# A decoder kernel: head outputs turned into both partition halves, context keys and values in pairs of row halves, and biases as three bf16 rows

## The chip, the cores and the metric

The kernel runs on one core of a Trainium2 chip. The metric is the device time of one execution in microseconds. The engines are named as in the profile: PE is TensorE's matmul, PEld its weight load, DVE is VectorE, ACT is ScalarE, POOL is GpSimd, SP is SyncE, whose queue issues nearly all the loads. TensorE's clock is throttled by the chip; the profile gives the granted clock as a share of full speed.

## The reference, cut to what matters

The program is a decoder of two layers on `x` of 4 x 256 x 256 fp32 values and a context `ctx` of 4 x 256 x 64. Each layer adds three blocks to `x`, each on a layer norm of it. Layer 0 has a latent attention, a cross attention and a block that works on the tokens a router picks. Layer 1 has a *head attention*, a causal cross attention, and 28 experts of which each token takes six. The change touches the head attention and the context side of the cross attention in layer 1:

```python
# head attention of layer 1: within a token, 16 heads attend to one another
qkv = x @ w_qkv.T + b_qkv                     # x: layer norm of the input, (4, 256, 256)
q, k, v = qkv.reshape(b, n, 3, 16, 16) ...    # (b, n, head, dim)
attn = softmax(einsum('bnhd,bngd->bnhg', q, k) / sqrt(256))
out = einsum('bnhg,bngd->bnhd', attn, v)
out = out.transpose(0, 2, 1, 3).reshape(b, n, c)   # a head's tokens become rows
return out @ w_out.T + b_out

# cross attention of layer 1 (two groups of 512 tokens, 16 heads of 16)
qp = q @ Wq.T
k, v = split(latent_kv @ Wkv_expand.T)        # latent_kv: ctx, 64 values per token
scores = qh @ kh.T / 4, causal; attn = softmax(scores)
return (attn @ vh) @ Wout.T
```

The reshape after the head attention's transpose mixes tokens and heads: row n' = 16 h + q of its result holds head h of the 16 tokens 16 q to 16 q + 15. So the result of all heads of all tokens of a batch row must be turned before the output projection.

## The kernel before, in words

The 1024 tokens lie as eight tiles `x[t]` of 128 rows by 256 values in SBUF through the whole program; each block reads them and adds to them. Blocks are written as Python generators that yield between steps, and `_side_by_side` deals the steps of two of them out in turn, by the numbers of steps that it is given. Each engine then has one in-order queue; within what the data and the buffers allow, the framework's scheduler may set an instruction earlier or later than it was written. PSUM has three rings of two buffers: tag `sc` (two banks each), `tp` and `o`. What takes a buffer of a ring waits until the user before the last has been read out.

*Head attention* (`_head_attention`, L1331 to L1462) works in two halves of four tiles, `half(0)` and `half(1)`. In each half the layer norm is turned into `hT` (L1361 to L1371) with the tokens ordered so that a step j takes 128 tokens whose heads share columns. Then four steps j:

- `project(j)` (L1375): a product of one row, the ones times the bias (L1380), and two of 128 rows (L1382), into a `sc` buffer `pqkv`, for each of two column halves of 384. Two ScalarE copies bring it to `qkv` (L1386).
- `weigh(j)` (L1389): GpSimd multiplies queries by keys, four products of 128 x 1024 (`qk`, L1400). VectorE sums two of them at a time (L1406), takes the maximum and subtracts (L1409, L1410). ScalarE takes the exponential (L1411).
- `combine(j)` (L1414): VectorE divides by the sum, multiplies by the values (`pv`, L1425) and sums into `O` (L1432).

The steps overlap: `weigh(j + 1)` goes before `combine(j)`. After the fourth step `O` holds 16 heads of 4 x 16 values; for each four heads (n = 0 to 3) four fp32 transposes against the identity bring 64 rows each to a `tp` buffer `o_tp` (L1446) and one ScalarE copy of 64 x 512 sorts them into `aoT` (L1448). The output projection of each tile is a one-row bias product (L1453) and four products of 64 rows (L1456) into an `o` buffer `apo`; VectorE adds it to `x` (L1457). There are four such tiles per half.

*Cross attention* (`_cross_attention`, L1465) loads its weights first (L1478 to L1485) in SyncE's queue. `context_kv(bp)` (L1494), once for each half of the tokens, fills `vz` with zeros by two DMAs (L1499), makes four key products of 64 rows by 512 columns (`xpk`, L1502) with a ScalarE copy each into `kz` (L1503), and four value products of 64 rows by 256 columns (`xpv`, L1510), two to a `tp` buffer, with two ScalarE copies to every other column of `vz` (L1515). The queries are `xpq` (L1646) and `xqT` (L1647); scores go to `sc` buffers `xsc`.

The order around the change (L532 to L584): the head attention's loads are issued and its half 0 (`heads_a`) is dealt out beside layer 0's cross attention of the second half of the tokens (`mix`) and the routed block on it; that ends in the `mpb` turns and the update of `x`. Then `heads_a`'s remaining steps and the cross attention of the first tokens are dealt out beside `second()`: eight steps of `heads_b` (half 1 of the head attention), both `context_kv`, and the rest of `heads_b`. After that comes the cross attention of the second tokens, and the experts.

Constants lie in one tile `cst`: the identity, masks, ones and others at columns named `K_...`.

Of the kernel before, what the change touches and what calls it, by code (L numbers as in the profile page):

```python
# [54 lines left out]
K_END = K_LATER + P  # L55
# [52 lines left out]
def kernel(ctx: ExitStack, tc: tile.TileContext, w: dict, out: bass.AP):  # L108
# [310 lines left out]
    for _ in range(4):  # L419
# [17 lines left out]
        blank=blank, psum=psum, sm=sm, cst=cst, ident=ident, identb=identb, maskb=maskb, tri=tri, ones=ones,  # L437
# [550 lines left out]
def _routed_block(nc, w, x, env):  # L988
# [20 lines left out]
    for i in range(4):  # L1009
        nc.gpsimd.tensor_copy(later[:, i], cst[:, K_LATER:K_END])  # L1010

# [319 lines left out]
def _head_attention(nc, tc, x, w, env):  # L1331
# [5 lines left out]
    ident, ones_row, layernorm = (env[n] for n in ("ident", "ones_row", "layernorm"))  # L1337
# [7 lines left out]
    b1qkv = a1.tile([1, 3 * C], F32, name="b1qkv")  # L1345
    nc.sync.dma_start(b1qkv, w["a_bqkv"])
    w1out = a1.tile([4 * D, 4, C], F32, name="w1out")
    nc.sync.dma_start(w1out, w["a_wout"].rearrange("(m p) n -> p m n", p=4 * D))
    b1out = a1.tile([1, C], F32, name="b1out")
    nc.sync.dma_start(b1out, w["a_bout"])  # L1350

    def half(g):
# [22 lines left out]
        def project(j):  # L1375
            qkv = a2.tile([P, 3 * C], F32, tag="qkv", name="qkv")
            pq = psum.tile([P, 2, 512], F32, tag="sc", name="pqkv")
            for i in range(2):
                cols = slice(i * 384, (i + 1) * 384)
                nc.tensor.matmul(pq[:, i, :384], ones_row, b1qkv[:, cols], start=True, stop=False)  # L1380
                for k in range(2):
                    nc.tensor.matmul(  # L1382
                        pq[:, i, :384], hT[:, k, j * P : (j + 1) * P], w1qkv[:, k, cols], start=False, stop=(k == 1)
                    )
            for i in range(2):
                nc.scalar.copy(qkv[:, i * 384 : (i + 1) * 384], pq[:, i, :384])  # L1386
            return qkv
# [54 lines left out]
        oT = a1.tile([4 * D, 4, 2, H, Q], F32, tag="oT", name="aoT")  # L1442
        for n in range(4):
            tp = psum.tile([P, 4, P], F32, tag="tp", name="o_tp")
            for i in range(4):
                nc.tensor.transpose(tp[: 4 * D, i, :], O[:, 4 * n + i].rearrange("p j d -> p (j d)"), ident)  # L1446
            dst = oT[:, :, :, 4 * n : 4 * n + 4, :].rearrange("p m b h q -> p h (m b) q")
            nc.scalar.copy(dst, tp[: 4 * D].rearrange("p h (m q) -> p h m q", q=Q))  # L1448
            yield
        for t in range(4):  # L1450
            b, i = divmod(t, 2)
            po = psum.tile([P, C], F32, tag="o", name="apo")
            nc.tensor.matmul(po, ones_row, b1out, start=True, stop=False)  # L1453
            for m in range(4):
                lhsT = oT[:, m, b, 8 * i : 8 * i + 8, :].rearrange("p h q -> p (h q)")
                nc.tensor.matmul(po, lhsT, w1out[:, m, :], start=False, stop=(m == 3))  # L1456
# [8 lines left out]
def _cross_attention(nc, tc, x, w, env):  # L1465
# [4 lines left out]
    psum, sm, ctxT = (env[n] for n in ("psum", "sm", "ctxT"))  # L1470
# [9 lines left out]
    wxk = c1.tile([LAT, 4, P], F32, name="wxk")  # L1480
    nc.sync.dma_start(wxk, w["c_wk"])
    wxv = c1.tile([LAT, C], F32, name="wxv")
    nc.sync.dma_start(wxv, w["c_wv"])
# [10 lines left out]
    def context_kv(bp):  # L1494
# [5 lines left out]
        for n in range(4):  # L1500
            pk = psum.tile([P, 512], F32, tag="tp", name="xpk")
            nc.tensor.matmul(pk, wxk[:, n], ctxT[:LAT, tok], start=True, stop=True)  # L1502
            nc.scalar.copy(kz[:, n // 2, n % 2, :], pk)  # L1503
            if n % 2:
                yield
        for t in range(0, 4, 2):
            pv = psum.tile([P, 2, C], F32, tag="tp", name="xpv")
            for j in range(2):
                t0 = (4 * bp + t + j) * P
                nc.tensor.matmul(pv[:, j], ctxT[:LAT, t0 : t0 + P], wxv, start=True, stop=True)  # L1510
# [172 lines left out]
def _constants():  # L1683
# [23 lines left out]
    c[:, K_LATER:] = np.where(p[None, :] <= SLOTS + p[:, None] % SLOTS, 0.0, -1e30)  # L1707
# [3 lines left out]
def _laid_out(a):  # L1711


    def row(v):
        return v.reshape(1, -1)
# [42 lines left out]
    o["a_bqkv"] = by_dim(a["L1_attn_b_qkv"].reshape(-1, 1)).reshape(1, -1)  # L1758
    o["a_wout"] = a["L1_attn_w_out"].T
    o["a_bout"] = row(a["L1_attn_b_out"])  # L1760
# [34 lines left out]
```

## Time and profile before

| what | value |
|---|---|
| time, median of 3 runs | 945.69 us (944.62 to 947.14) |
| the profiled execution, its own time | 917.45 us |
| its span, first to last instruction | 915.7 us |
| mean granted TensorE clock | 0.842 |
| VectorE busy, ScalarE busy | 522.6 us (57%), 293.6 us (32%) |

The profiled execution was 28 us shorter than the timed median; its span lacks 1.75 us of its own time.

These are the stages around the change, with the busy time of each engine in them and the granted clock, from the trace:

| stage, us from the start | PE | DVE | ACT | POOL | clock |
|---|---|---|---|---|---|
| 290 to 330: start of heads half 0, mix | 29.1 | 23.1 | 9.4 | 6.3 | 0.64 |
| 330 to 440: heads half 0 beside the routed block | 66.2 | 88.8 | 17.9 | 48.3 | 0.73 |
| 440 to 465: turns of half 0, first step of half 1, first keys and values | 21.3 | 8.5 | 9.4 | 10.9 | 0.84 |
| 465 to 492: output projections, keys and values, second step | 26.7 | 14.0 | 4.1 | 1.0 | 0.50 |
| 492 to 560: steps of half 1 beside the cross attention | 48.4 | 45.2 | 20.4 | 27.6 | 0.75 |
| 560 to 604: end of half 1, its projections | 40.8 | 37.2 | 18.4 | 0.7 | 0.82 |
| 604 to 692: cross attention of the second tokens | 72.8 | 52.0 | 35.6 | 38.0 | 0.82 |

A line of the profile names the instruction's line in the code, engine, operation, output and inputs by the program's names, the shape of the array used for products (64*128: 64 rows, 128 columns), and how many instructions it stands for. An fp32 product is two instructions on TensorE, two passes over the same columns; "x8" for four products is that. In the order of time, `[5.44 <-PE pqkv L1382]` after an instruction says that its engine had been idle for 5.44 us and that the named instruction released it. Idle time of an engine that nothing waits for costs nothing.

### The profile page before, as it was taken

What the parts mean: (1) busy time and instruction counts of PE and PEld (TensorE: products, weight loads), DVE (VectorE), ACT (ScalarE), POOL (GpSimd) and SP (SyncE); (2) the same over time, 40 slices, a digit from 0 to 9 for tenths busy, and PEclk for the clock granted to TensorE, in tenths of its full rate; (3) what the DMA queues carried; (4) which work ended last, traced back from release to release, by engine and by line L of the source; (5) the groups of instructions that cost most, each with busy time, mean ns of one, the idle gap of its engine ahead of it and who ended that gap; (6) DMA issues with size and microseconds to landing.
All of it is one profiled execution on the core that took longest, in us unless ns stands there. A gap on an engine that the chain in (4) does not pass through costs nothing. (4 is left out here: it accounts for less than half of the span.)

```text
span 915.7 us, 11540 instructions
## 1 busy us (share of the span) xinstructions
PE 735.1 (80%) x3594; PEld 460.5 (50%) x3594; DVE 522.6 (57%) x1304; ACT 293.6 (32%) x958; POOL 309.5 (34%) x248
## 2 busy tenths in 40 slices
PE   4999999779988696543988786989696589979990
PEld 2645656445455343331554354656464367757770
DVE  3357467886553578779363678847554323353332
ACT  1245354442441211211220343416431134424430
POOL 2012122214210263740314222023532466646662
PEclk9799999889999678667767677879966889989995
DMA  8769999500505100510300000057216756676655
GB/s 318 208 221 325 325 325 336 216 1 0 184 6 212 59 3 4 180 46 0 124 0 0 1 1 1 1 223 297 79 46 176 213 94 116 110 206 111 111 80 155
DMA packets 84270, 117.03 MB, mean 128 GB/s; under 512 B 5133, under 2 KB 72271, under 8 KB 83696
## 3 DMA queue, kind: packets, MB, share of 16 engines
q1 hardware_dynamic: 71312, 99.46, 33.3%
q0 software_dynamic: 11232, 15.21, 9.8%
q10 hardware_dynamic: 1664, 1.57, 0.5%
q8 instruction: 33, 0.54, 0.2%
q14 instruction: 29, 0.24, 0.1%
HBM read 58.80 MB, written 55.33 MB: 125 GB/s over the span
## 5 line engine op out<-in xcount | busy, mean ns | idle before, releaser
L883 POOL DMA_INDIRECT acc<-ys,xb x62 | 97.8, 1578 | 76.2 <-ACT Tx L839 43.7
L1400 POOL TENSOR_TENSOR qk<-qkv 128x1024 f32<-128x1024 f32 x32 | 74.3, 2352 | 71.9 <-ACT qkv L1386 71.9
L333 POOL TENSOR_TENSOR pr<-pr,rs 128x512 f32<-128x512 f32 x32 | 41.5, 1298 | 162.6 <-DVE rs L331 81.9
L847 PE MATMUL pgu<-wgu_e,Tx 128*128 x248 | 91.9, 496 | 2.9 <-ACT Tx L839 1.6
L323 ACT ACTIVATE pr<-sc,nb 128x256 f32<-128x256 f32 x128 | 59.0, 474 | 60.2 <-DVE nb L318 59.9
L878 PE MATMUL py<-wdn_e,Th 88*128 x248 | 65.2, 389 | 9.8 <-issue 9.3
L1544 ACT ACTIVATE xpr<-xsc,cnm 128x256 f32<-128x256 f32 (+1 forms) x128 | 52.2, 421 | 63.6 <-DVE cnm L1539 50.7
L701 POOL DMA_INDIRECT lists<-R,rows x48 | 46.7, 973 | 59.0 <-DVE rows L685 19.5
L878 PEld LDWEIGHTS py<-wdn_e,Th 88*128 88x128 f32 x248 | 47.7, 195 | 26.2 <-issue 9.8
L1406 DVE TENSOR_REDUCE s<-qk 128x128 f32<-128x2048 f32 x16 | 36.6, 2286 | 42.2 <-POOL qk L1400 42.1
L847 PEld LDWEIGHTS pgu<-wgu_e,Tx 128*128 128x128 f32 x248 | 45.2, 202 | 20.5 <-issue 4.1
L853 DVE TENSOR_TENSOR eh<-pgu,sg 128x176 f32<-128x176 f32 x62 | 21.1, 340 | 51.3 <-ACT sg L851 51.3
L93 PE MATMUL av<-pT,ckt 128*64 128x256 f32 x256 | 40.5, 412 | 8.7 <-DVE pT L349 8.5
L314 DVE TENSOR_REDUCE nm<-sc 128x4 f32<-128x1024 f32 x32 | 38.9, 1217 | 13.1 <-PE sc L93 13.0
L882 ACT ACTIVATE ys<-py,wsel 128x256 f32<-128x256 f32 x62 | 29.4, 475 | 48.7 <-PE py L878 45.7
L867 DVE SCALAR_TENSOR_TENSOR wjunk<-cst,e_all,xb 128x28 f32<-128x28 f32 x62 | 15.2, 247 | 49.6 <-ACT ys L882 48.7
L851 ACT ACTIVATE sg<-pgu 128x176 f32<-128x176 f32 x62 | 19.7, 318 | 73.9 <-PE pgu L847 73.9
L93 PE MATMUL xsc<-kz,xqT 32*128 32x256 f32 (+1 forms) x256 | 37.5, 402 | 7.3 <-ACT xpr L1544 4.3
L96 PE MATMUL tp<-cst,pr 128*128 128x128 f32 x256 | 38.7, 293 | 3.3 <-DVE pT L349 2.4
L93 PE MATMUL sc<-ckv,qk 64*128 64x256 f32 x256 | 39.3, 405 | 1.5 <-ACT qk L301 0.7
L96 PE MATMUL x_tp<-cst,xpr 128*128 128x128 f32 x192 | 36.2, 322 | 4.3 <-DVE xpT L1560 2.6
L96 PEld LDWEIGHTS tp<-cst,pr 128*128 128x128 f32 x256 | 29.8, 148 | 17.4 <-issue 14.1
(334 smaller groups left out, 1529.4 us busy)
## 6 DMA issues: line engine op xcount, KB each, us to landing
lists<-blank SPq DMA_DIRECT2D x9, 3600.0 KB, 28.1
wgu_e<-in_e_gu_dram SPq DMA_DIRECT2D x4, 2464.0 KB, 25.6
xb<-lists SPq DMA_DIRECT2D x62, 144.0 KB, 2.9
acc<-blank SPq DMA_DIRECT2D x5, 1152.0 KB, 11.6
wdn_e<-in_e_dn_dram SPq DMA_DIRECT2D x4, 1232.0 KB
wq<-in_m_wq_dram SPq DMA_DIRECT2D x4, 1024.0 KB, 11.3
mwo<-in_m_wo_dram SPq DMA_DIRECT2D x2, 2048.0 KB
part<-acc SPq DMA_DIRECT2D x16, 256.0 KB, 3.2
```

Of the source, the lines that this page charges most:

```text
L93: self._next(self.engine.matmul(*args, **kw))
L96: self._next(self.engine.transpose(*args, **kw))
L314: nc.vector.tensor_reduce(nm, sc, AX.X, ALU.max, negate=True)
L323: nc.scalar.activation(pr[:, e, qt, :], sc[:, e, qt, :], AF.Exp, bias=nb[:, e, qt : qt + 1], accum_out=ss[:, e, qt : qt + 1],)
L333: nc.gpsimd.tensor_tensor(pr[:, 1], pr[:, 1], rs[:, 1].unsqueeze(2).to_broadcast([P, 2, S]), ALU.mult)
L701: put = nc.gpsimd.indirect_dma_start(out=lists, out_offset=bass.IndirectOffsetOnAxis(ap=rows[:, i, n : n + 1], axis=0), in_=R[:, i, :], in ...
L847: nc.tensor.matmul(pg, xT[:, k, :], self.wgu[:, bass.ds(e * (4 * M) + k * 2 * M, 2 * M)], start=(k == 0), stop=(k == 1))
L878: nc.tensor.matmul(py, hT[:, k, :], self.wdn[:, bass.ds(e * (2 * C) + k * C, C)], start=(k == 0), stop=(k == 1))
L883: nc.gpsimd.indirect_dma_start(out=accs[self.puts % len(accs)], out_offset=bass.IndirectOffsetOnAxis(ap=xb[:, C : C + 1].bitcast(I32), axi ...
L1400: nc.gpsimd.tensor_tensor(pr[:, 4 * i : 4 * i + 4], q3[:, h0 : h0 + 4].unsqueeze(2).to_broadcast([P, 4, H, D]), k3.unsqueeze(1).to_broadca ...
L1406: nc.vector.tensor_reduce(s[:, hh], pr, AX.X, ALU.add)
L1544: nc.scalar.activation(pr[:, j, cols], sc[:, j, cols], AF.Exp, bias=nm[:, i, j : j + 1], accum_out=ss[:, i, h : h + 1])
```

## The change

It has three parts.

*The turn and the output projection.* Each head group of `O` is multiplied twice, as fp32 matrix products instead of transposes: by the identity into partitions 0 to 63 of `o_tp` and by a new constant, the identity with its columns rolled by 32 (`turned32`, 128 more columns of `cst`), into partitions 64 to 127. So both partition halves hold the turned heads, the upper half with the column blocks moved by 32. Two ScalarE copies of 128 rows (one per m) instead of one of 64 sort them into an `aoT` of 128 rows, and the output projection is two products of 128 rows instead of four of 64. `w1out` is loaded to match.

*Biases.* Both bias vectors are one array of 1024 values, loaded as 128 x 8. VectorE rounds it to bf16, subtracts, rounds the rest, subtracts and rounds again: three bf16 parts. Three DMAs write them to DRAM, one reads them back as three rows of 1024. The bias product is then three bf16 rows of ones (`onesb`) against three bf16 rows of bias, in both projections.

*Context keys and values.* The context and the two weights are loaded twice, into partitions 0 to 63 and 64 to 127 (six loads in place of two; `ctxT`, loaded at the start, stays for layer 0). Products alternate between the two halves, so that two in a row use different rows of the array. They take `sc` buffers, two banks each, instead of `tp`; keys are copied two products at a time.

```diff
-K_END = K_LATER + P
+K_TURN = K_LATER + P
+K_END = K_TURN + P
...
-    b1qkv = a1.tile([1, 3 * C], F32, name="b1qkv")
-    nc.sync.dma_start(b1qkv, w["a_bqkv"])
-    w1out = a1.tile([4 * D, 4, C], F32, name="w1out")
-    nc.sync.dma_start(w1out, w["a_wout"].rearrange("(m p) n -> p m n", p=4 * D))
-    b1out = a1.tile([1, C], F32, name="b1out")
-    nc.sync.dma_start(b1out, w["a_bout"])
+    bias = a1.tile([P, 8], F32, name="b1")
+    nc.sync.dma_start(bias, w["a_b"].rearrange("(p c) -> p c", p=P))
+    b1 = a1.tile([3, 4 * C], BF16, name="b1rows")
+    scratch = env["stack"].enter_context(tc.tile_pool(name="b1d", bufs=1, space=DRAM)).tile([3, 4 * C], BF16, name="b1d")
+    for i in range(3):
+        part = a1.tile([P, 8], BF16, name=f"b1part{i}")
+        nc.vector.tensor_copy(part, bias)
+        if i < 2:
+            nc.vector.tensor_tensor(bias, bias, part, ALU.subtract)
+        nc.sync.dma_start(scratch[i].rearrange("(p c) -> p c", p=P), part)
+    nc.sync.dma_start(b1, scratch)
+    onesb = a1.tile([3, P], BF16, name="onesb")
+    nc.vector.tensor_copy(onesb, env["ones"][:3])
+    b1qkv, b1out = b1[:, : 3 * C], b1[:, 3 * C :]
+    w1out = a1.tile([P, 2, C], F32, name="w1out")
+    nc.sync.dma_start(w1out, w["a_wout"].rearrange("(m p) n -> p m n", p=P))
...
-                nc.tensor.matmul(pq[:, i, :384], ones_row, b1qkv[:, cols], start=True, stop=False)
+                nc.tensor.matmul(pq[:, i, :384], onesb, b1qkv[:, cols], start=True, stop=False)
...
-        oT = a1.tile([4 * D, 4, 2, H, Q], F32, tag="oT", name="aoT")
+        oT = a1.tile([P, 2, 2, H, Q], F32, tag="oT", name="aoT")
         for n in range(4):
             tp = psum.tile([P, 4, P], F32, tag="tp", name="o_tp")
             for i in range(4):
-                nc.tensor.transpose(tp[: 4 * D, i, :], O[:, 4 * n + i].rearrange("p j d -> p (j d)"), ident)
-            dst = oT[:, :, :, 4 * n : 4 * n + 4, :].rearrange("p m b h q -> p h (m b) q")
-            nc.scalar.copy(dst, tp[: 4 * D].rearrange("p h (m q) -> p h m q", q=Q))
+                head = O[:, 4 * n + i].rearrange("p j d -> p (j d)")
+                nc.tensor.matmul(tp[: 4 * D, i, :], head, ident, start=True, stop=True)
+                nc.tensor.matmul(tp[4 * D :, i, :], head, env["turned32"], start=True, stop=True)
+            for m in range(2):
+                dst = oT[:, m, :, 4 * n : 4 * n + 4, :].rearrange("p b h q -> p h b q")
+                src = tp[:, :, m * 2 * 32 : m * 2 * 32 + 32].rearrange("p h (b q) -> p h b q", q=Q)
+                nc.scalar.copy(dst, src)
             yield
         for t in range(4):
             b, i = divmod(t, 2)
             po = psum.tile([P, C], F32, tag="o", name="apo")
-            nc.tensor.matmul(po, ones_row, b1out, start=True, stop=False)
-            for m in range(4):
+            nc.tensor.matmul(po, onesb, b1out, start=True, stop=False)
+            for m in range(2):
                 lhsT = oT[:, m, b, 8 * i : 8 * i + 8, :].rearrange("p h q -> p (h q)")
-                nc.tensor.matmul(po, lhsT, w1out[:, m, :], start=False, stop=(m == 3))
+                nc.tensor.matmul(po, lhsT, w1out[:, m, :], start=False, stop=(m == 1))
...
-    wxk = c1.tile([LAT, 4, P], F32, name="wxk")
-    nc.sync.dma_start(wxk, w["c_wk"])
-    wxv = c1.tile([LAT, C], F32, name="wxv")
-    nc.sync.dma_start(wxv, w["c_wv"])
+    ctx2 = c1.tile([P, B * S], F32, name="ctx2")
+    wxk = c1.tile([P, 4, P], F32, name="wxk")
+    wxv = c1.tile([P, C], F32, name="wxv")
+    for dst, src in ((wxk, "c_wk"), (wxv, "c_wv"), (ctx2, "ctxT")):
+        for e in range(2):
+            nc.sync.dma_start(dst[e * LAT : (e + 1) * LAT], w[src])
...
-        for n in range(4):
-            pk = psum.tile([P, 512], F32, tag="tp", name="xpk")
-            nc.tensor.matmul(pk, wxk[:, n], ctxT[:LAT, tok], start=True, stop=True)
-            nc.scalar.copy(kz[:, n // 2, n % 2, :], pk)
-            if n % 2:
-                yield
+        for g in range(2):
+            pk = psum.tile([P, 2, 512], F32, tag="sc", name="xpk")
+            for e in range(2):
+                half = slice(e * LAT, (e + 1) * LAT)
+                nc.tensor.matmul(pk[:, e], wxk[half, 2 * g + e], ctx2[half, tok], start=True, stop=True)
+            nc.scalar.copy(kz[:, g], pk)
+            yield
         for t in range(0, 4, 2):
-            pv = psum.tile([P, 2, C], F32, tag="tp", name="xpv")
+            pv = psum.tile([P, 2, 512], F32, tag="sc", name="xpv")
             for j in range(2):
                 t0 = (4 * bp + t + j) * P
-                nc.tensor.matmul(pv[:, j], ctxT[:LAT, t0 : t0 + P], wxv, start=True, stop=True)
+                half = slice(j * LAT, (j + 1) * LAT)
+                nc.tensor.matmul(pv[:, j, :C], ctx2[half, t0 : t0 + P], wxv[half], start=True, stop=True)
+            pv = pv[:, :, :C]
...
-    c[:, K_LATER:] = np.where(p[None, :] <= SLOTS + p[:, None] % SLOTS, 0.0, -1e30)
+    c[:, K_TURN:] = np.roll(np.eye(P), -(P // 4), 1)
+    c[:, K_LATER:K_TURN] = np.where(p[None, :] <= SLOTS + p[:, None] % SLOTS, 0.0, -1e30)
```

More of the change, by code (lines that the diff above doesn't have):

```diff
@@ L436 @@
     env = dict(
-        blank=blank, psum=psum, sm=sm, cst=cst, ident=ident, identb=identb, maskb=maskb, tri=tri, ones=ones,
+        turned32=cst[:, K_TURN:], blank=blank, psum=psum, sm=sm, cst=cst, ident=ident, identb=identb, maskb=maskb, tri=tri, ones=ones,
         ones_row=ones_row, layernorm=layernorm, ln_stats=ln_stats, ln_apply=ln_apply, rsqrt=rsqrt, transposed=transposed, ctxT=ctxT, neghalf=neghalf,
@@ L1009, in _routed_block @@
     for i in range(4):
-        nc.gpsimd.tensor_copy(later[:, i], cst[:, K_LATER:K_END])
+        nc.gpsimd.tensor_copy(later[:, i], cst[:, K_LATER:K_TURN])
     kT = ms1.tile([P, HK, 2 * SLOTS], F32, name="mkT")
@@ L1336, in _head_attention @@
     psum, sm = env["psum"], env["sm"]
-    ident, ones_row, layernorm = (env[n] for n in ("ident", "ones_row", "layernorm"))
+    ident = env["ident"]
     H = D = 16
@@ L1465, in _cross_attention @@
 def _cross_attention(nc, tc, x, w, env):
-    psum, sm, ctxT = (env[n] for n in ("psum", "sm", "ctxT"))
+    psum, sm = env["psum"], env["sm"]
     ident, identb, maskb, ln_apply, transposed = (env[n] for n in ("ident", "identb", "maskb", "ln_apply", "transposed"))
@@ L1757, in _laid_out @@
     o["a_wqkv"] = by_dim(a["L1_attn_w_qkv"]).T
-    o["a_bqkv"] = by_dim(a["L1_attn_b_qkv"].reshape(-1, 1)).reshape(1, -1)
+    o["a_b"] = np.concatenate([by_dim(a["L1_attn_b_qkv"].reshape(-1, 1)).ravel(), a["L1_attn_b_out"]])
     o["a_wout"] = a["L1_attn_w_out"].T
-    o["a_bout"] = row(a["L1_attn_b_out"])
     o["c_wq"] = a["L1_xattn_Wq"].T
```

## The prediction

> **What bounds the kernel now.** I read first the page's busy table and its 40 slices (22.9 us each), to see which stages the change touches and what is full there.
>
> ```profile
> PE 735.1 (80%) x3594; PEld 460.5 (50%) x3594; DVE 522.6 (57%) x1304; ACT 293.6 (32%) x958; POOL 309.5 (34%) x248
> ...
> PE   4999999779988696543988786989696589979990
> ...
> DVE  3357467886553578779363678847554323353332
> ...
> PEclk9799999889999678667767677879966889989995
> ```
>
> The touched lines run from 289 to 604 us (slices 13 to 26). There TensorE's granted clock is mostly 0.6 to 0.8, and no engine is full throughout: VectorE leads before 440, TensorE from 440 to 490. So the stage must be read by waits. For the tile `qkv` (what each engine waited for, who waited):
>
> ```profile
>   PE pqkv L1382: 31.2, 6
> ...
>   POOL qk L1400: 71.9, 7
> ...
>   DVE s L1406: 42.1, 14
> ```
>
> GpSimd's products (four of 2.33 us per step) start when ScalarE has copied a projection, and VectorE's sums follow them. A late projection therefore holds GpSimd, then VectorE. Third, the order of time around the two longest such waits:
>
> ```profile
> 465.29 2.07 PE L1502 MATMUL xpk<-ctxT,wxk 64*128 64x512 f32 x2 [2.90 <-ACT vz L1515]
> ...
> 473.56 3.78 PE L1456 MATMUL apo<-w1out,aoT 64*128 64x256 f32 x8
> ...
> 480.12 3.78 PE L1456 MATMUL apo<-w1out,aoT 64*128 64x256 f32 x8
> ...
> 487.11 1.64 PE L1380 MATMUL pqkv<-b1qkv,cst 1*128 1x384 f32 x2
> ...
> 491.73 0.86 ACT L1386 COPY qkv<-pqkv 128x384 f32<-128x384 f32 x2 [5.44 <-PE pqkv L1382]
> ...
> 499.60 0.68 DVE L1647 TENSOR_SCALAR xqT<-xpq 128x512 f32<-128x512 f32 x1
> ...
> 510.48 1.64 PE L1380 MATMUL pqkv<-b1qkv,cst 1*128 1x384 f32 x2
> ...
> 519.52 0.86 ACT L1386 COPY qkv<-pqkv 128x384 f32<-128x384 f32 x2 [5.93 <-PE pqkv L1382]
> ...
> 520.46 9.20 POOL L1400 TENSOR_TENSOR qk<-qkv 128x1024 f32<-128x1024 f32 x4 [18.52 <-ACT qkv L1386]
> ```
>
> From 465 to 491 TensorE works without a gap and everyone waits: GpSimd stands from 461 to 492.7 but for 1 us, VectorE is half idle. The queue is in order, so the second projection of heads half 1 and the front of the next block stand behind output projections and context keys. And it runs at half clock, as the stretches show (busy us of PE, PEld, DVE, ACT, POOL; clock; DMA share):
>
> ```profile
> 456.00:460.00 4.00, 4.00 (x21) 2.96 (x20) 2.29 (x1) 3.07 (x6) 4.00 (x3) 1.00 0.00 0
> ...
> 472.00:476.00 4.00, 4.00 (x9) 2.47 (x9) 2.25 (x2) 0.59 (x1) 0.00 (x0) 0.50 0.00 0
> ...
> 480.00:484.00 4.00, 4.00 (x10) 3.14 (x10) 0.12 (x2) 0.00 (x0) 0.00 (x0) 0.50 0.00 0
> ```
>
> **The change, part by part** (gains negative; times are those of the profile before).
>
> *Prices.* A 384-column fp32 product is two passes of 0.64 us at half clock or 0.32 at full; 256 columns 0.43 or 0.21; 512 columns 0.85 or 0.43 (start-to-start in the rows above and their neighbours). A bf16 product is one pass, and by the mask row (128x512 bf16, 0.38 us alone, pipeline included) a quarter of the stream: 0.32 us for 384 columns at half clock where fp32 took 1.6. Products in two row halves: eight 64*128 passes of 256 columns of the first attention's scores go in 1.06 us start to start, where 8 x 0.213 is 1.7, so 1.6 times as fast. In two column halves (av, 128*64): eight in 1.02, 1.7 times.
>
> *A. Bias rows, 289 to 323.* New on SyncE's queue: one bias load for two, three writes to DRAM, one read back. The third write is issued when VectorE has made the third row. VectorE's six small operations stand between the layer norms at 298 to 301 and cost 0.07 to 0.17 each (rows of such size), about 0.6 in all. The second half of the wq load now stands behind those writes: 302 instead of 292.7, and first needed at about 362, so its cover is 50 us. Write and read back: 2.8 us each by wxv's landing, plus at most 3.1 for the wq half in front (1 MB at 336 GB/s, the highest slice): rows ready at 308 to 311. In the new order the first bias product stands after psim (about 311) and before transposes that wait until 316 to 319. Hidden; without this cover each us late stands in TensorE's queue 1:1. What is gained: the old bias products stood earlier, and held the transposes behind them:
>
> ```profile
> 301.74 2.92 PE L1380 MATMUL pqkv<-b1qkv,cst 1*128 1x384 f32 x4
> ...
> 304.60 1.54 PE L468 MATMUL h_tp<-cst,h 128*128 128x128 f32 x6
> ```
>
> Their inputs were there at 301.6, so up to -2.9; less 0.6 of VectorE, and the psim behind them ran at full clock already at 310 and may now fall into the half-clock part (+0.4 to +1.7). I take -2.0 (ends -2.5 and 0).
>
> *B. First projection, 322 to 330.* One bias at half clock, 1.6 to 0.3, lies between the transposes and qkv at 329.79, which starts GpSimd's first eight products: -1.3.
>
> *C. 330 to 440.* The scheduler also moves one `qk` product ahead of a rotation on GpSimd. One side: sums earlier by 2 us; other side: the routed block's third turn later by 1.7. VectorE orders both; -0.5 (ends -1 and +2).
>
> *D. o_tp and the first projection of half 1, 444 to 452.* Each turn becomes two fp32 products of two passes, 128 columns each: 16 passes for 4. By av's 1.7, 16 x 0.107 / 1.7 = 1.0 us at full clock for 0.43, four times a half. Seven of the eight products of n=0 stand ahead of the projection, at half clock: +1.2, less the bias's 0.5: +0.7. ScalarE's aoT copies become 16 of 128 elements: 0.25 us by the 128x128 kv copy (0.27) for 8 x 0.58, equal in sum.
>
> *E. 452 to 500.* The stall 461 to 465 stays: ScalarE's exp at 464.29 waits for GpSimd's products, vz copies stand behind it, and key and value products now share the "sc" buffers, whose third user waits for those copies. From 465.3 before: 40 fp32 passes and 6 bias passes, 26.1 us. After: xpk one pair 4 x 0.85 / 1.6 = 2.1; apo 8 x 0.43 = 3.4 (two row groups for four); xpv 8 x 0.43 / 1.6 = 2.1; pqkv 8 x 0.64 = 5.1 (none is done ahead now); four biases 1.1; gaps 1.2: 15.0 at half clock. The projection ends at 480.4 for 491.4: -11. Not all of it is path: in GpSimd's new order two of its products (4.7) precede cln_rs, and VectorE's order puts two sums (2.3 each) ahead of hT and xqT. Following it through: copy 481.4, two products 486.1, cln_rs 487.1, four products 491.7, sum 494.0, hT 494.7, first half of xpq 496.4, xqT 497.1 for 499.6 to 500.3: -3.1, with one sum done beforehand. If the clock is full from about 470, the projection ends at 475 and xqT comes at 491.7: -8.6. I take -6.
>
> Here two rules of the Trainium skill are weighed. "TensorE: Matmul & The Clock Gate", Part 1, has the clock full after one busy window of about 3.4 us. The rows differ: 26 us busy at 0.50 from 465 on, full only after projections and transposes of all 128 rows; while 448 to 460, entered through such products, is at 1.00. By the page the clock would be full from 469 whatever the change, 26.1 would have been about 15, and E would be worth some 3; by the rows E's work at half clock is real, and full-row products (apo, paired keys) may end it sooner. I go by the rows. "TensorEngine Tiling (Array Packing)", Key Properties, says that a change of tiling mode drains the array, which speaks against the change: between the first o_tp and xpq I count 29 changes of mode for 20, and o_tp cuts one key pair apart. The rows price it: xpk 453.74 follows o_tp and pqkv that began at 452.53 with 1.07 us of streaming, so about 0.1 per change: +1, within E's gap term.
>
> *F. Third projection, 508 to 520.* Two biases at half clock, 3.2 to 0.6, ahead of the copy that GpSimd awaits 18.5 us: -2.6. *G.* The fourth, at full clock: -1.3, but VectorE is full from 560 to 580: 0.
>
> *H. Tail, 581 to 604.* VectorE's last sum of O ends at 583.8; then TensorE is the path to x_in at 603.56. At full clock: four output projections of 1.7 become 0.85 (-3.4), biases 4 x 0.6 to 0.15 (-1.8), o_tp +0.6 x 4 (+2.4), and for the last two tiles nothing else stands between: -3.
>
> *Context loads.* Four more loads (0.7 MB) ahead of wxo and the vz fills: +2.5 us of issue, +2 of transfer. ctx2 lands at about 447 for a use at 451, vz at 453 for 458: hidden. The constants' extra 64 KB: 0.2 us at the early loads' 318 GB/s; 0. After 604 nothing is changed: it shifts.
>
> Sum: -2.0 -1.3 -0.5 +0.7 -6 -2.6 -3 = -14.7, on a profiled execution of 917.45 (span 915.7 and 1.75 around it): 902.7. The timed median is 945.69, 28.2 higher; I take the gain over in us: **931.0**.
>
> **Rivals.** (1) *The clock comes back early*: E is -8.6, H holds, A and C at their good ends, F under a full clock -1.3, and VectorE's two sums done ahead pay later (-4): about -22, 924. For: apo and keys fill all rows. Against: 485 to 491 was full-row and stayed at half. (2) *The gain is lost among the other queues*: VectorE and GpSimd have fixed orders and each projection awaits the buffer of the one before; then only B, F and half of H stay: -6, 940. For: VectorE at 10 of 10 from 560 to 580. Against: GpSimd's long waits name qkv. (3) *The pairs don't pair* (o_tp stands between the halves, drains): xpk and xpv cost 8.5 instead of 4.2 after 465, no effect on B, F, H: -10, 936. (4) *Slower: the gate closes in the tail.* From 580 to 600 TensorE is busy 18.9 of 20 us at clock 1.00. With a fifth of that gone, gaps may open; at half clock the remaining 17 us cost up to 17 more. The gains ahead of it are about 12, so it decides once 12 of the 17 run at half; all of it gives +2 to +5, 949. For: 0.66 reigned at 560 to 580. Against: cross attention's own products keep TensorE busy there.
>
> **How the numbers follow.** Forecast with (3), -9 to -19: 0.50; (1) 0.14; (2) 0.14; no difference, a delay eating all: 0.06; (4) or a late bias row: 0.16. Within 0.3% (2.8 us, about what a measurement can tell from no change) is 0.06, faster 0.78, slower 0.16. Range: from (1) with 3 us more, 921, to just above the old median, 947, leaving out most of (4): 0.17 outside.
>
> **What would show it.** B and F: biases of one pass, qkv copies earlier against their transposes by 1.3 and 2.6. E: the second projection's copy at 477 to 482 after allowing for the shift of A to C, and GpSimd's wait before it at 16 to 21 us for 31. H: last apo to x_in, 2 us of TensorE for 6. A: b1rows landed before psim ends, no wait of TensorE on a DMA at the first bias. Wrong if TensorE waits there, if o_tp takes over 1.5 us per four turns at full clock, or if the clock in 580 to 605 falls below 0.8.

## The result, and the profile after

The changed kernel takes **935.26 us** (median of 4 runs, 933.27 to 937.99), the kernel before 946.02 (944.62 to 947.14). The ratio is 0.989, with a 95% interval of 0.985 to 0.993: 10.8 us faster, where 14.7 were forecast (931.0, range 921 to 947). Executions of one kernel on one chip spread by 1 to 2%, and those of the biases alone, below, fall into two groups (seven at 912 to 918 us, seven at 923 to 933), so that their ratio stands between the two.

The profiled execution after took 933.27 us, its span is 931.5: longer than the 915.7 of before, although the kernel is faster. The first profile of before shows an execution like those of set A below, where that kernel takes 921 us; the timed runs of before took 946. The difference lies after 604 us, where the two kernels are alike. Up to there the two traces can be compared stage by stage.

The busy table and slices of the changed kernel's page (its slices are 23.3 us):

```profile
PE 716.2 (77%) x3634; PEld 447.2 (48%) x3634; DVE 533.2 (57%) x1310; ACT 291.9 (31%) x962; POOL 310.3 (33%) x248
...
PE   4998999789988667334857778879665689969990
...
DVE  3367457886553599878278579537334233353332
...
PEclk9899989889998588567866778869766799989995
```

TensorE is busy 19 us less. VectorE is busy 10.6 us longer, and only 0.6 of that was expected. The waits around the tile `qkv`, as before:

```profile
  PE pqkv L1394: 25.4, 6
...
  POOL qk L1412: 92.2, 7
  DVE s L1418: 39.5, 10
```

ScalarE waits 5.8 us less for projections, yet GpSimd's waits for ScalarE's copies sum to 20 us more. Most of that is an old wait under another name. In before, GpSimd's operation of the next block's layer norm (`cln_rs`) came ahead of the products of the second step, and 24.5 us of idle time ended at it, released by VectorE:

```profile
485.51 1.01 POOL L134 TENSOR_TENSOR cln_rs<-ln_ve,neghalf 128x4 f32<-128x4 f32 x1 [24.50 <-DVE ln_ve L145]
492.73 9.21 POOL L1400 TENSOR_TENSOR qk<-qkv 128x1024 f32<-128x1024 f32 x4 [6.21 <-ACT qkv L1386]
```

Now two products come first, and the idle time, shorter by 12 us in all, ends at ScalarE's copy. The order of time around the second projection of half 1 after the change:

```profile
466.76 1.25 PE L1524 MATMUL xpk<-ctx,wxk 64*128 64x512 f32 x4 [3.35 <-ACT vz L1538]
...
468.26 2.08 PE L1473 MATMUL apo<-w1out,aoT 128*128 128x256 f32 x4
...
470.27 1.23 PE L1532 MATMUL xpv<-wxv,ctx 64*128 64x256 f32 x4
...
474.91 0.49 PE L1392 MATMUL pqkv<-b1rows,onesb 3*128 3x384 bf16 x1
...
480.01 0.86 ACT L1398 COPY qkv<-pqkv 128x384 f32<-128x384 f32 x2 [4.33 <-PE pqkv L1394]
480.94 4.60 POOL L1412 TENSOR_TENSOR qk<-qkv 128x1024 f32<-128x1024 f32 x2 [18.45 <-ACT qkv L1398]
485.50 1.01 POOL L135 TENSOR_TENSOR cln_rs<-ln_ve,neghalf 128x4 f32<-128x4 f32 x1
...
487.78 4.16 DVE L151 TENSOR_SCALAR h<-x_in,ln_mv,cln_rs 128x256 f32<-128x256 f32 x4
489.01 0.69 PE L164 MATMUL h_tp<-cst,h 128*128 128x128 f32 x2 [9.11 <-DVE h L151]
...
498.58 0.69 DVE L1670 TENSOR_SCALAR xqT<-xpq 128x512 f32<-128x512 f32 x1 [1.87 <-PE xpq L1669]
```

The projection's copy comes at 480.0 for 491.7, much as worked out. Then TensorE stands from 480 to 489: the layer norm of the next block waits on GpSimd behind two products of the head attention, and the queries `xqT` come at 498.6 for 499.6. Nearly all of an 11 us gain is gone within one step in this trace.

So that executions can be compared, the table counts from the first product of `mpb` at the start of the stage (294 to 298 us in all of them). Three traces of before and three of after, from the sets below:

| us from the first `mpb` product | before | after |
|---|---|---|
| first projection's copy, half 0 | 35.7, 35.7, 35.7 | 32.1, 32.0, 29.9 |
| first projection's copy, half 1 | 156.7, 155.6, 156.7 | 155.7, 156.5, 157.6 |
| second projection's copy, half 1 | 197.6, 196.5, 197.6 | 183.4, 185.8, 186.8 |
| first `xqT` | 205.5, 204.3, 205.5 | 202.0, 204.4, 205.4 |
| third projection's copy, half 1 | 225.4, 224.3, 225.4 | 217.4, 219.8, 220.8 |
| end of the last sum of `O` | 289.7, 288.7, 289.8 | 280.5, 283.6, 284.5 |
| end of the last addition to `x` | 309.9, 307.9, 309.9 | 296.7, 299.8, 300.7 |

The last row is 10.1 us earlier on the mean (299.1 for 309.2); the timed gain is 10.8.

### The profile page after: what moved, and what is told of

It is laid out like the page before. It is cut to its first block, busy times and chain, and to the rows that moved or that the text cites. A ratio compares the mean times of both kernels' runs of the same rounds, so it can differ in the third digit from the quotient of the medians.

```text
span 931.5 us, 11640 instructions
## 1 busy us (share of the span) xinstructions
PE 716.2 (77%) x3634; PEld 447.2 (48%) x3634; DVE 533.2 (57%) x1310; ACT 291.9 (31%) x962; POOL 310.3 (33%) x248
## 4 chain that ended last, share of the span: by engine, by line
PE 38%; DVE 25%; DMA 14%; POOL 8%; issue 6%; ACT 6%; another core or an unknown queue 1%; SPq 1%; ACTq 0%; DVEq 0%; POOLq 0%
DMA acc<-ys,xb 10%; POOL qk L1412 5%; ACT pr L324 4%; PE xsc L94 3%; PE pgu L848 3%; PE po L94 2%; DVE pv L1437 2%; PE x_tp L97 2%; PE pq L94 2%; DVE s L1418 2%; DVE pr L333 2%; PE pqkv L1394 2%; PE av L94 2%; PE py L879 2%; DVE O L1444 2%
## 5 line engine op out<-in xcount | busy, mean ns | idle before, releaser
L97 PE MATMUL x_tp<-cst,xpr 128*128 128x128 f32 x192 | 39.7, 345 | 12.5 <-DVE cnt L753 4.3
L94 PE MATMUL av<-pT,ckt 128*64 128x256 f32 x256 | 40.1, 408 | 10.1 <-DVE pT L350 9.9
L97 PEld LDWEIGHTS x_tp<-cst,xpr 128*128 128x128 f32 x192 | 27.6, 176 | 22.0 <-issue 9.0
```

The source lines that it names most:

```text
L94: self._next(self.engine.matmul(*args, **kw))
L97: self._next(self.engine.transpose(*args, **kw))
```

## The experiments

They ran in three sets, each on another chip with its own runs of before: set A (before 921.54 us, 35 runs), set B (945.81, 17 runs), set C (947.70, 11 runs). Ratios are to before in the same set.

**Before, twice more**, unchanged: `b_again` in set A, `b_third` in set C.

> The kernel before, unchanged, for a second trace of it, since the first one shows an execution of 917 us where the timed ones take 946. Theory (the difference lies in the granted clock and its timing, behind the changed stage): up to the last addition of head attention, at 603.6 us in the first trace, this execution is within 4 us of the first one, and what it has more comes after. Rival (the typical execution is longer inside the changed stage, 290 to 604): that addition comes 8 us or more later.

> The kernel before, unchanged, a third trace, from whichever chip this set falls on. Theory (the 28 us between the first trace and the median of 946 are the chip's): on a chip where the timed runs of before take about 946 us, head attention still ends at 602 to 604 us in this trace, and from there to the first expert it takes 125 to 135 us in place of 102; on a chip with 921 us that stage takes 102. Rival (the changed stages are longer on the slower chip too): head attention ends at 608 or later there.

They took 915.8 and 942.5 us. Head attention ended at 602.8 and 606.1 us; counted from the first `mpb` product that is 307.9 and 309.9, for 309.9 in the first trace. From there to the first expert's product it was 101.8 and 123.4 us (101.5 in the first trace), and from that product to the last instruction of the compute engines 200 to 208 us in every trace. So the chips differ in that one stage. The rival's 608 did not come, though 606.1 and 123.4 lie just outside the 602 to 604 and the 125 to 135 that the theory named. What VectorE waited for between 606 and 730 us, in the first trace of before and then in `b_third` (total us, times, longest):

```profile
DVE R L150 <- POOL ln_rs L134: 9.2, 3, 7.4
DVE cnm L1538 <- PE xsc L93: 6.3, 11, 1.6
```

```profile
DVE cnm L1538 <- PE xsc L93: 10.6, 9, 4.0
DVE xpT L1560 <- remote: 7.6, 2, 4.4
DVE x_in L1600 <- remote: 6.1, 1, 6.1
...
DVE cnt L752 <- remote: 4.4, 1, 4.4
```

"remote" stands for a releaser that the profile can't name. The sum of such waits of VectorE in that stage is 0 in the four traces of set A and the first profile of before, and 13 to 21 us in the nine others; the stage takes 101 to 104 us in the former and 123 to 134 in the latter. What it is stays open. It weighs on both kernels.

**One part alone, on the kernel before** (set A): the biases (`bias_only`), the turn and output projection (`turn_only`), the context keys and values (`ctx_only`). Each takes its hunks of the diff shown above and leaves the rest; `bias_only`, for example:

```diff
-    b1qkv = a1.tile([1, 3 * C], F32, name="b1qkv")
-    nc.sync.dma_start(b1qkv, w["a_bqkv"])
+    b1 = a1.tile([3, 4 * C], BF16, name="b1rows")
+    ...
-                nc.tensor.matmul(pq[:, i, :384], ones_row, b1qkv[:, cols], start=True, stop=False)
+                nc.tensor.matmul(pq[:, i, :384], onesb, b1qkv[:, cols], start=True, stop=False)
```

> The kernel before with the bias rows alone. By the prediction's steps: A -2.0, B -1.3, two bias products' worth of E (five of 0.6 to 1.6 us less, half of it path) -1.8, F -2.6, of H the biases' -1.8: about -9 us. Rival (the order of GpSimd and VectorE eats what a shorter projection gives): B and F alone stand, -4. Rival (rows arrive late or the reordering costs): 0 or above.

> The kernel before with the turn into both halves and the output projection of 128 rows alone. By the prediction's steps: D +1.2, of E the output projections' 5.2 at half clock, half of it path, -2.6, H -3.4 +2.4 = -1.0: about -2.5 us. Rival (the gate comes back early through products of all rows): -6 or more, with the granted clock above 0.8 from 470 to 490. Rival (the turns cost more than the projections give): +1 to +3.

> The kernel before with context keys and values in pairs of row halves alone. By the prediction's steps: of E 4.3 us at half clock, half of it path: about -2.3 us. Rival (the pairs don't overlap): 0, with two key products of 512 columns still 1.7 us apart at half clock. Rival (the shared score buffers turn into a wait of the next projection or of the scores): +1 to +4, with an idle TensorE before a projection that names a copy of keys or values.

| alone | ratio to before | interval |
|---|---|---|
| biases | 0.999 | 0.995 to 1.002 |
| turn | 1.001 | 0.998 to 1.003 |
| context | 0.990 | 0.986 to 0.994 |

Context gave three to four times what was expected of it (-9 us by the ratio and -7 by the medians, for -2.3), the biases nothing that can be told from zero (for -9), the turn nothing (for -2.5). In the traces, one execution each, head attention ends 303.2 us from the first `mpb` product with the biases, 315.9 with the turn and 303.5 with the context, for 307.9 to 309.9 before: there the biases and the context gain 5 to 6 us each, and the turn costs about 7.

**One part taken back, from the changed kernel** (set B), with the changed kernel itself:

```diff
# no_ctx: context keys and values of before      no_bias: fp32 one-row biases
# no_turn: 64-row turn, four products of 64 rows per output projection
-            for m in range(2):
+            for m in range(4):
                 lhsT = oT[:, m, b, 8 * i : 8 * i + 8, :].rearrange("p h q -> p (h q)")
```

> The changed kernel, unchanged, beside its parts. In its first trace head attention ends 10.7 us earlier than before (592.9 for 603.6), but the next stages, where the two kernels have the same instructions in the same order, take 29 us longer up to the first expert (130.7 for 101.8). Theory (those 29 us are the state of the chip of that execution, which the timed runs of before had too, and no effect of the change): here the changed kernel is 10 to 15 us faster than before, and from head attention's end to the first expert takes 100 to 106 us. Rival (the change makes the later stages longer by how it leaves the clock): it gains 5 us or less here, and that stage takes over 115 us.

> The changed kernel with the context keys and values of before. Alone, that part gave 0.990 and the two others nothing that could be told from zero. Theory (context keys and values carry the gain because they are what stands in TensorE's queue at half clock and what the row copies wait for; the rest is taken back by the order of GpSimd and VectorE): within 3 us of before. Rival (the prediction's sum: the parts add, context about -2.3): 8 to 12 us faster than before.

> The changed kernel with the fp32 one-row biases of before. Theory (context carries the gain): 8 to 10 us faster than before, as context alone. Rival (the prediction's sum, biases about 9 of the 14.7): 4 to 6 us faster than before.

> The changed kernel with the 64-row turn and output projection of before. Theory (context carries the gain, biases add what they gave alone): 9 to 12 us faster than before. Prediction's sum: 12 us faster. Rival (a part of the gain comes only when all stand together, since the projection that waits stands behind all of them): 5 us or less.

| set B | median us | ratio to before | interval |
|---|---|---|---|
| changed kernel | 934.04 | 0.986 | 0.981 to 0.991 |
| without context pairs | 935.28 | 0.989 | 0.984 to 0.994 |
| without bias rows | 938.43 | 0.993 | 0.989 to 0.996 |
| without the turn | 931.54 | 0.983 | 0.978 to 0.987 |

The changed kernel's stage from head attention to the experts took 133.8 us, for 130.3 in its first trace: the theory's 100 to 106 was wrong for this chip, since before is as slow there. The theory that context alone carries the gain falls too: without it 1.1% of gain is left. So does the plain sum: the biases, worth nothing alone, are worth some 0.6% when the rest is in. The intervals overlap, though, there and for the turn, which by the medians is better left out.

The traces say more than these times. The step of `xqT` shown above, from the second projection's copy to the first `xqT`, divides the kernels into groups:

| kernel | second copy to `xqT`, us | products of that step ahead of `cln_rs` | first copy of half 1 to `xqT`, us |
|---|---|---|---|
| before (three traces) | 7.9 | none | 48.8 |
| biases alone; context alone | 7.9 | none | 46.0; 42.1 |
| without bias rows; without the turn (two traces) | 7.9 | none | 40.3; 37.0 and 37.4 |
| turn alone; the changed kernel (three traces) | 18.6 | two | 54.3; 46.3 to 47.9 |
| without context pairs | 18.9 | three | 44.4 |

Where GpSimd runs products first, the step is 10.7 to 11 us longer. No kernel without the turn has it; of those with the turn only the one without bias rows escapes it. The last column shows why the parts can't add in this stage. Biases and context together (without the turn) take 11 to 12 us off it; with the turn on top, 9 to 11 of these are lost. Where the order stays as it was (without bias rows), the turn takes off 1.8 more than context alone.

The traced execution of `no_turn` took 943.8 us, with its tail at half clock, so its later stages are not compared; it prices a rival, below.

**GpSimd's order put back** (`cln_first`, set C), with `no_turn` and the changed kernel as measures. The one edit to the changed kernel, made where the four products of step 1 of half 1 are issued, is an order without data:

```diff
+                    if (g, j) == (1, 1):
+                        tc.add_manual_dep(done.ins, env["marks"]["cln"], ...NoSync..., reason="layer norm first")
```

> The changed kernel, with GpSimd's order of before at one place: the layer norm's power for the cross attention (cln_rs) goes ahead of the four products of the second step of half 1, where the change put two of those products first. Theory (two products of 4.7 us on GpSimd and a sum on VectorE in front of the layer norm are what took the gain of E): the first queries are out at 487 to 491 us for 498.6, the third projection's copy at 503 to 506 for 514, the last sum of O ends 6 to 9 us earlier than in the changed kernel, and it is 6 to 9 us faster than the changed kernel, unless TensorE's clock stays at a half after 570: then the tail takes 12 us more and it gains nothing. Rival (VectorE's own sequence sets the end of half 1, whatever comes first): the last sum ends within 2 us of the changed kernel's.

> The changed kernel with the turn and output projection of before, once more, since its one trace ran from 566 to 602 at half clock while its fastest times were the lowest on that chip. Theory (half 1 is 8 us earlier than in the changed kernel because cln_rs goes first, and the tail is either at full clock, about 20 us, or at half clock, about 33): executions in two groups some 12 us apart, the faster one 3 to 8 us faster than the changed kernel. Rival (its tail is slow in general, since the biases' gaps were what kept the clock up): its median no better than the changed kernel's.

> The changed kernel, unchanged, as the measure for the two others on the same chip. Theory: 0.985 to 0.990 of before, with the end of head attention at 592 to 597 us. Rival (the gain depends on the chip): within 0.5% of before here.

| set C | median us | ratio to before | interval |
|---|---|---|---|
| changed kernel | 937.11 | 0.986 | 0.981 to 0.992 |
| with `cln_rs` first | 930.17 | 0.982 | 0.978 to 0.986 |
| without the turn | 929.06 | 0.982 | 0.978 to 0.986 |

By these ratios both others are some 4 us faster than the changed kernel, where 6 to 9 (`cln_first`) and 3 to 8 (`no_turn_2`) were expected; the intervals overlap, so the times alone don't prove it. The traces show the step: the last sum of `O` ends 275.4 and 275.5 us from the first `mpb` product, against 280.5 to 284.5 in the changed kernel, and the last addition ends at 293.7 and 293.8 against 296.7 to 300.7. The fairest measure is the first trace of the changed kernel, which `cln_first` equals to 0.1 us up to the second copy of half 1 (183.4): against it the last sum of `O` is 5.1 us earlier and the last addition 3.0. The rival of `cln_first` (VectorE's own sequence sets the end) falls. The two groups of executions expected of `no_turn_2` did not show: its runs lie between 926 and 933. Nor did all of the first expectation come true: `xqT` in `cln_first` is at 493.7, not at 487 to 491, for `h` took long and `xpq` behind it ran at a mean clock of 0.58 (6.32 us). The order of time there:

```profile
480.00 1.01 POOL L137 TENSOR_TENSOR cln_rs<-ln_ve,neghalf 128x4 f32<-128x4 f32 x1 [17.27 <-DVE ln_ve L150]
481.04 7.41 DVE L155 TENSOR_SCALAR h<-x_in,ln_mv,cln_rs 128x256 f32<-128x256 f32 x4 [1.12 <-POOL cln_rs L137]
481.25 9.40 POOL L1416 TENSOR_TENSOR qk<-qkv 128x1024 f32<-128x1024 f32 x4 [0.24 <-ACT qkv L1402]
...
493.70 0.69 DVE L1681 TENSOR_SCALAR xqT<-xpq 128x512 f32<-128x512 f32 x1 [2.45 <-PE xpq L1680]
```

and in `no_turn_2`, where `cln_rs` has 3.4 us until the products begin:

```profile
481.07 1.01 POOL L134 TENSOR_TENSOR cln_rs<-ln_ve,neghalf 128x4 f32<-128x4 f32 x1 [16.83 <-DVE ln_ve L145]
482.11 1.38 DVE L150 TENSOR_SCALAR h<-x_in,ln_mv,cln_rs 128x256 f32<-128x256 f32 x4 [1.12 <-POOL cln_rs L134]
...
484.51 9.19 POOL L1411 TENSOR_TENSOR qk<-qkv 128x1024 f32<-128x1024 f32 x4 [2.44 <-ACT qkv L1397]
...
491.37 0.68 DVE L1664 TENSOR_SCALAR xqT<-xpq 128x512 f32<-128x512 f32 x1
```

The same four operations of VectorE take 1.38 us with GpSimd idle and 7.41 beside its products: after the first one, each gets through once per product (the transposes that wait for them begin at 481.5, 483.9, 486.2 and 488.5 us).

## Why the prediction was right in its sum and wrong in its steps

The direction and the range held, with 10.8 of the 14.7 us. By its own steps (us, negative is a gain; each trace of after against the first trace of before, in the order of the table of marks):

| step | forecast | measured, three traces | mean |
|---|---|---|---|
| A + B, to the first copy of half 0 | -3.3 | -3.6, -3.7, -5.8 | -4.4 |
| C, from there to the last `mpb` addition | -0.5 | +1.3, +3.0, +6.4 | +3.6 |
| D, to the first copy of half 1 | +0.7 | +1.3, +0.5, +0.3 | +0.7 |
| E, to the second copy of half 1 | -11 | -13.2, -11.6, -11.7 | -12.2 |
| E, what is left of it at `xqT` | -6 | -2.5, -0.9, -1.0 | -1.5 |
| F, from `xqT` to the third copy | -2.6 | -4.5, -4.5, -4.5 | -4.5 |
| G and the rest, to the last sum of `O` | 0 | -1.2, -0.5, -0.6 | -0.8 |
| H, from there to the last addition | -3 | -4.0, -4.0, -4.0 | -4.0 |
| sum, with E as left at `xqT` | -14.7 | -13.2, -10.1, -9.2 | -10.8 |

Two terms were too good by 8.6 us together: C, and E behind the projection. A + B, F and H each gave 1 to 2 us more than forecast and hid nearly half of that, so the sum came out better than its parts, in part by luck. Which trace of before is taken matters too: against `b_again`, C comes out 1.4 us worse and the gain in sum 2.0 us smaller.

**A and B were right, a little small.** The rows were back in time: read back from 305.8, first used at 313.0, with no wait of TensorE on a load, and the second half of the wq load was issued at 302.8, as worked out. A 3-row bf16 bias costs 0.26 to 0.33 us at the pipeline's pace, where the fp32 one took 1.6 at half clock.

**C was the first wrong step**, by 1.8 us in the first trace and by 4 on the mean of the three. The lead of after's first trace over before is 3.6 us at the fourth sum `s` (54.4 us from the first `mpb` product for 58.0), 3.1 at the first sum of the second step (81.0 for 84.1), and 1.3 at that step's first `pv` (93.8 for 95.0). In between, products that start earlier run beside other operations of VectorE. The order of time of before, then of after:

```profile
372.96 0.74 DVE L1153 TENSOR_TENSOR t<-qf,tab 128x256 f32<-128x256 f32 x2
373.54 6.91 POOL L1400 TENSOR_TENSOR qk<-qkv 128x1024 f32<-128x1024 f32 x3 [0.83 <-ACT qkv L1386]
...
380.40 1.55 DVE L1220 SCALAR_TENSOR_TENSOR x_in<-ha,passed,x_in 128x256 f32<-128x256 f32 x1
...
384.19 2.29 DVE L1406 TENSOR_REDUCE s<-qk 128x128 f32<-128x2048 f32 x1 [1.57 <-POOL qk L1400]
```

```profile
371.27 2.90 DVE L1154 TENSOR_TENSOR t<-qf,tab 128x256 f32<-128x256 f32 x2
...
371.42 2.47 POOL L1412 TENSOR_TENSOR qk<-qkv 128x1024 f32<-128x1024 f32 x1 [1.45 <-ACT qkv L1398]
...
375.25 6.88 POOL L1412 TENSOR_TENSOR qk<-qkv 128x1024 f32<-128x1024 f32 x3
...
379.80 4.01 DVE L1221 SCALAR_TENSOR_TENSOR x_in<-ha,passed,x_in 128x256 f32<-128x256 f32 x2
...
384.40 2.27 DVE L1418 TENSOR_REDUCE s<-qk 128x128 f32<-128x2048 f32 x1
```

In before the two `t` take 0.74 us and the products begin just behind them; in after a product begins at 371.42, in the midst of the pair, and it takes 2.90. That costs nothing, for VectorE then waits for products. But two `x_in` in a row take 4.01, and the sum behind them starts as they end, though its products were done at 382.1; in before it waited for its products. There the lead is lost. VectorE is the fullest engine here: from 330 to 440 us it is busy 96.7 of 110 us, for 88.8 in before. Most of the growth of its busy time is no new work, but the same work held up: four `spread` take 4.2 us more in sum, four `x_in` 2.1 and six `t` 1.9.

The clearest case is one that cost nothing. The first copy of half 0, 3.6 us earlier in the stage's own time, starts the products just before VectorE's last two `spread` operations instead of behind them (before, then after):

```profile
329.04 0.47 DVE L1043 TENSOR_SCALAR spread<-cst,ha 128x128 f32<-128x128 f32 x2
330.79 2.33 POOL L1400 TENSOR_TENSOR qk<-qkv 128x1024 f32<-128x1024 f32 x1 [4.87 <-ACT qkv L1386]
```

```profile
329.63 6.92 POOL L1412 TENSOR_TENSOR qk<-qkv 128x1024 f32<-128x1024 f32 x3 [3.03 <-ACT qkv L1398]
329.71 4.63 DVE L1044 TENSOR_SCALAR spread<-cst,ha 128x128 f32<-128x128 f32 x2
```

Two operations that take 0.47 us together take 4.63. The longest `spread` is 2.36 us in every kernel with the new biases and 0.28 in every one without. But before's VectorE had nothing to do there except wait for products, so the 4.2 us were absorbed.

Before's own first trace could have given the price. Two operations on 128 x 4 values, `chosen`, take 2.4 us each in it; in `b_again`, the same program, they pass in 0.15 and 0.16, and the fourth sum `s` comes at 56.3 us for 58.0 (before, then `b_again`):

```profile
342.25 2.38 DVE L1070 TENSOR_TENSOR chosen<-rank 128x4 f32<-128x4 f32 x1
...
346.85 2.36 DVE L1071 TENSOR_SCALAR chosen<-chosen 128x4 f32<-128x4 f32 x1
```

```profile
343.06 0.15 DVE L1070 TENSOR_TENSOR chosen<-rank 128x4 f32<-128x4 f32 x1
...
347.64 0.16 DVE L1071 TENSOR_SCALAR chosen<-chosen 128x4 f32<-128x4 f32 x1
```

That the three traces of after differ in C, from +1.3 to +6.4, is the granted clock. The first and the second agree to 0.1 us up to the products `mgu` of the routed block, 120.5 us from the first `mpb` product; these take 5.01 us at a mean clock of 0.72 in the one and 6.67 at 0.54 in the other, and what follows is 1.7 us later. In the third the first copy of half 0 comes 2.2 us earlier, at a clock of 0.94 for 0.61 from 28 to 32 us, and the next steps don't keep it; then the products `pv<-wkv` run at 0.57 for 1.00 from 68 to 76 us, the second step's first `pv` comes 2.0 us later, and `mgu` runs at 0.59. So of C's mean of +3.6, 2.3 us go with the clock of two executions.

The Trainium skill states the mechanism ("SBUF — State Buffer", section "SBUF: two separate sides"): VectorE and GpSimd share a pair of ports, and a VectorE operation in a two-port mode, or with two inputs in SBUF, finds it locked for the whole of a GpSimd instruction that started first. The rows of `t` and `x_in`, which have two inputs, agree with it. Whether `spread` and `h`, with one tensor input, run in such a mode no run here shows; that they are held up is measured. So each VectorE operation of the kinds shown, where it meets a 2.33 us product, is to be priced at up to a whole product and not at its own 0.3 to 0.8; the prediction's C priced the moved products alone, and none of the operations that they would meet.

**E was right at the projection and wrong behind it.** Followed through, it had two products first and `xqT` done at 497.1, that is -3.1; then I took -6, halfway to a clock that comes back early. That halving is the step that failed. The trace took the path as followed up to `hT`, which is copied by 494.7 as forecast. But TensorE had stood for 9.1 us, the granted clock is 0.50 from 488 to 498, and `xpq` runs at it, so that `xqT` is done at 499.3. `xpq` in before, then in after:

```profile
493.58 3.70 PE L1646 MATMUL xpq<-hT,wxq 128*128 128x512 f32 x8 [0.68 <-ACT hT L166]
```

```profile
494.83 5.43 PE L1669 MATMUL xpq<-hT,wxq 128*128 128x512 f32 x8 [1.94 <-issue]
```

In the five traces with products first, `xpq` takes 5.4 to 5.9 us at a mean clock of 0.62 to 0.67; in the eight with GpSimd's order as it was, 3.70 at 1.00. That `h` was held up by the products (4.16 us for 1.38) cost less: the sum behind it starts 0.7 us after its products end.

`cln_first` shows what that order cost: one edit, and the last sum of `O` comes 5.1 us earlier. The order appears only in kernels with the turn. That the scheduler chose it because the turn lengthened the path to the layer norm's input is presumed, not shown. D's own cost was right (a turn of 16 passes, 1.03 us at full clock for 1.0 forecast), but it was priced on TensorE alone; the price of the order that came with it was booked in E, and halved there.

The clock behaved as the rows of before said, not as the rule of the Trainium skill ("TensorE: Matmul & The Clock Gate", Part 1) that the prediction weighed. The stretches of after:

```profile
468.00:472.00 4.00, 4.00 (x12) 2.07 (x12) 4.00 (x3) 1.47 (x3) 0.00 (x0) 0.50 0.00 0
472.00:476.00 4.00, 4.00 (x10) 2.03 (x11) 3.25 (x9) 0.83 (x3) 0.00 (x0) 0.50 0.00 0
476.00:480.00 4.00, 3.90 (x9) 1.44 (x7) 3.67 (x4) 0.00 (x0) 0.00 (x0) 0.76 0.00 0
480.00:484.00 4.00, 0.00 (x0) 0.00 (x0) 0.00 (x0) 0.86 (x2) 3.06 (x2) 1.00 0.00 0
```

TensorE is busy from 466.8, falls to half clock at about 468 and is at full clock again from about 478, some 10 us at half, although half of that work has all rows. Rival (1) falls, and E's work at half clock was real.

**F and H were right in kind and too small.** F's two biases and a clock that rises inside the third projection give -4.5. In H the last projections cost 1.1 us at full clock and the turns 1.0. **The pairs pair**: four passes of `xpv` take 1.16 us at half clock, start to start, where four single ones take 1.84 in before; rival (3) falls. Rival (2), the gain lost among the other queues, is the one that came in part: it names the mechanism, not the place.

**Rival (4)** did not decide here: in the three traces of after the clock is 1.00 from 580 to the end of the block. It is real, though. In the traced execution of `no_turn` TensorE is at half clock from about 567 to 602 us, the end of the block, while in `no_turn_2` the tail runs at full clock (the stretches of the one and of the other):

```profile
590.00:596.00 6.00, 6.00 (x17) 3.78 (x16) 2.84 (x18) 1.62 (x8) 0.00 (x0) 0.50 0.00 0
```

```profile
583.00:589.00 6.00, 6.00 (x35) 4.58 (x35) 4.65 (x24) 2.69 (x12) 0.00 (x0) 1.00 0.01 3
```

From the last sum of `O` to the last addition it is 33.9 us in the one and 18.3 in the other: 15.6 us, against "up to 17" in the prediction. What decides between the two stays open.

The gain in microseconds carried over from a profile of 917 us to runs of 946, because the 28 us between them lie in a stage that the change does not touch.

What stays open: why the parts don't add in the timed runs. In E the order of GpSimd explains it, by one trace of each kernel. But context is worth 7 to 9 us alone in set A and 1 to 2 us on top of the others in set B, and the sets differ in chip. What the second group of executions with the biases alone loses was not traced.

## What to carry to other kernels

When a change makes an engine's input ready earlier, list what the other engines do in exactly that microsecond: here products that came some 3 us earlier met VectorE operations that they had missed, and 1.8 us of a lead of 3.1 was given back. The trace of before can give that price: look there for operations that take several times their usual time. Follow a gain through each in-order queue to the next block's input before counting it; an order without data, one edit, kept 5 us at the end of the half there. Where TensorE has to stand in such a wait, price what follows at the lower clock as well. And before a profile is set against timed runs, look whether it shows an execution of their length, and if not, in which stage they differ.

## What the runs showed of the hardware that I had not expected

- Short VectorE operations on SBUF wait out whole GpSimd products: `spread` 2.36 us for 0.28, `h` up to 2.41 for 0.41, `chosen` of 128 x 4 values 2.38 for 0.15, `t` and `x_in` likewise. In the profile this is a longer duration, not a wait. VectorE's sums of 2048 columns keep their 2.29 us beside the same products.
- The same program takes 921 us on one chip and 946 to 948 on two others, all of it in one stage of some 100 us, with VectorE waits that have no named releaser (0 against 13 to 21 us).
- TensorE was at half clock from about 567 to 602 us in one execution of `no_turn`, although it was busy for 35.7 of the 36 us from 566 on.
- With TensorE idle from 479.9 to 489.0 us in after, the granted clock is 1.00 from 480 to 484 and 0.50 from 488 to 498.
